# A four-layer graph network on one core: the first layer's neighbour sums made a stage earlier and kept in DRAM, a group's first layer moved to another stage, lists and zeros moved

## The chip, the core and the metric

The kernel runs on one NeuronCore of a Trainium2 chip. The core has five engines, each with its own in-order instruction queue: TensorE (PE in the profile; its weight loads are PEld), VectorE (DVE), ScalarE (ACT), GpSimd (POOL) and SyncE (SP). SP computes nothing here: it issues transfers. ACT and POOL issue transfers too. All transfers of the core share 16 DMA engines. The metric is the time of one execution in microseconds (us); lower is better. The time before is the median of three runs.

## The reference

There are 32 batch entries of 512 nodes with 256 features each, and one 512 x 512 weighted adjacency matrix that is mostly zero. Four layers follow one another. Layers 0 and 3 have the same form with other weights, and the changed sums belong to layer 0:

```python
x0 = layer(x, adj, weights of L0)
def layer(h_t, A_a, A_m, W1, b1, W2, b2, Wa, ba, Wm, bm, beta1, beta2, beta3):
    pre_u = jnp.einsum('bud,dk->buk', h_t, W1[:d])
    pre_v = jnp.einsum('bvd,dk->bvk', h_t, W1[d:])
    hidden = jax.nn.relu(pre_u[:, :, None, :] + pre_v[:, None, :, :] + b1)
    S = jax.nn.sigmoid(jnp.einsum('buvk,ko->buvo', hidden, W2)[..., 0] + b2[0])
    a_t = jnp.einsum('buv,bud->bvd', S * A_a, h_t)
    m_t = jnp.einsum('uv,bud->bvd', A_m, h_t) * h_t
    return beta1 * h_t + beta2 * (a_t @ Wa + ba) + beta3 * (m_t @ Wm + bm)
# layer 1: x + relu((adj @ x) @ W + b)
# layer 2: dense attention over 512 nodes with adj added to the logits, then x + values + bias
# layer 3: layer(...) again with the weights of L3
```

`S` is needed only where the adjacency is not zero. The quantity `adj.T @ h`, multiplied by `h`, is the neighbour sum `m_t`; the kernel calls it `mhT` (it is held transposed).

## The kernel before

**Groups and stages.** The 32 entries are worked on in eight groups of four (`NB`). For each group `t` there are five kinds of work, each a Python generator that yields after a small piece:

- `first` (L755): per entry, load x into `h` (a pool with two buffers, tag "h"), transpose it on TensorE (`turned`, L549) to `hT`, store that to DRAM as `xT` (issued by ACT), and make the two projections `pre_u` and `pre_v` (`pre`, L560: matmuls at L570 and L572, VectorE at L574, L577 and L578, ScalarE at L575). Each 128 rows of them go to a DRAM table (`table<-puv`, issued by SP through `settle`).
- `edges` (L611) for layer 0, later again for layer 3. There are 36 items (`ITEMS`), each 128 neighbour slots for the four entries of the group. Per item POOL gathers rows of the table (`fetch`, L607), VectorE adds them to the node's own rows (L686), applies relu and multiplies by W2 (L694 for all four entries at once, with ScalarE summing at L672; or L702 per entry with the sum in the same instruction). Every few items a sigmoid is taken, and POOL scatters the results into a zeroed DRAM matrix `cells` (`put`, L601), of which there are two halves. Each scatter waits until the one before it into the same half has landed.
- `middle` (L788, `middle_one` L825): load the four row blocks of the cells (`SA`, `load` at L721), then for each entry: `mhT` (matmuls in L45 and product at L750), the aggregation with the scattered weights (`flat` copied by ScalarE at L809, matmuls at L840), the product with Wm (L847), `zT` (scaled by ScalarE at L845, added by VectorE at L848), layer 1 (L861, L45), layer 2's attention (L883 to L953; the four matmuls of L899 come once per entry), and the first projections for layer 3 (`pre` again).
- `last` (L1016): layer 3's sums for the group, with its own `mhT` (tag "mhT3").
- In group 0 `middle_before` (L773) makes `hWa` and `mhT` of layer 0 ahead of the stage, and the last group has `last_before` and `last_behind`.

**The order.** The pieces of all generators are interleaved by a table of times written by hand in `sparse_path` (L1079): `spread` and `edge_times` give each piece a due time in units of one middle stage, and `weave` (L444) runs them in that order. Streams of kind "fill" (`first` and `last`) aren't run at their due time but collected, and one or two are run whenever the middle stage yields a true value, which it does where it is about to wait. The middle stage of group t takes the time t-0.47 to t+0.53. `behind` (L495) ties an instruction of the edges to a place in its engine's queue behind the middle stage's pieces; a scheduler then fixes each engine's order at build time.

**Setup.** `Edges.build` (L249) makes the lists of neighbours. Its last part (from L345) finds, for nodes with more than eight neighbours, the "panels": it reads the counts with matmuls, gathers four tiles `got` from the DRAM tensor `lists` by indirect transfers (L368), and searches them (L374, L377). `zeros` (L534) clears the cells of layer 0 and, called by `zeros_behind`, those of layer 3: each time eight stores of 512 KB from one zeroed tile.

**Buffers named below.** Tiles of one tag share memory: "h1" and "hT1" hold x and its transpose for the middle stage, "eT" the attention weights and `flat`, "mhT0" also `feats`, "hWa0" also `zW`. At both ends of the kernel, `edges` borrows further tags as extra row buffers (`rows_more`).

Of the kernel before, what the change touches and what calls it, by code (L numbers as in the profile page):

```python
# [8 lines left out]
F32 = mybir.dt.float32  # L9
# [210 lines left out]
class Edges:  # L220
# [28 lines left out]
    def build(self, counts, adjT, lists, psum, big, tmp):  # L249
# [65 lines left out]
        acc, v, there, t = (sheet(NC * OWN) for _ in range(4))  # L315
        for c in (0, 2, 1, 3):
            at = slice(c, c + 1)
# [27 lines left out]
        js = slice(NC * OWN, ITEMS)  # L345
        pu = psum()[:, 0 : 2 * PANELS]
        ones_bf = bf2[:, 1024:1025]
        nc.vector.memset(ones_bf, 1.0)
        for k in range(2 * PANELS):
            h, q = divmod(k, PANELS)  # L350
            mm(nc, pu[:, k : k + 1], [(full[:, h * 2 + c, q * P : (q + 1) * P], ones_bf) for c in range(2)])
        u, node, slot, start, sp, v, there, t = (sheet(2 * PANELS) for _ in range(8))
        nc.vector.tensor_scalar(u, pu, float(HALF - 1), None, ALU.min)
        nc.vector.tensor_copy(node, u)
        nc.vector.tensor_scalar(node[:, PANELS:], u[:, PANELS:], float(HALF), None, ALU.add)
        inode = self.inode
        nc.vector.tensor_copy(inode, node)
        nc.vector.tensor_scalar(self.iu, node, 2.0, None, ALU.mult)
        nc.gpsimd.iota(slot, [[0, 2], [P, PANELS]], 0, 1, allow_small_or_imprecise_dtypes=True)
        nc.vector.tensor_scalar(start, u, float(N), None, ALU.mult)  # L360
        nc.vector.tensor_scalar(sp, slot, float(CELLS + NC // 2 * OWN * P), None, ALU.add)
        nc.vector.tensor_scalar(t, slot, 1.0, None, ALU.add)
        yield
        gots = []
        for k in range(2 * PANELS):
            gots.append(tmp.tile([P, 2 * N], F32, name=f"got{k}", tag=("h1", "hT1", "mhT0", "hWa0")[k]))
            index = bass.IndirectOffsetOnAxis(ap=inode[:, k : k + 1], axis=0)
            nc.gpsimd.indirect_dma_start(out=gots[k], out_offset=None, in_=lists, in_offset=index)  # L368
        yield
        for k in range(2 * PANELS):  # L370
            at = slice(k, k + 1)
            rank, adj = gots[k][:, 0:N], gots[k][:, N:]
            junk = bf2[:, 2048 + k % 2 * N :][:, 0:N]
            nc.vector.scalar_tensor_tensor(  # L374
                junk, rank, t[:, at], adj, ALU.is_equal, ALU.mult, accum_out=self.value_of(NC * OWN + k)
            )
            nc.vector.scalar_tensor_tensor(junk, rank, slot[:, at], ones, ALU.is_le, ALU.mult, accum_out=v[:, at])  # L377
            yield
        self.slots(js, v, there, t, start, sp, 0)
        yield  # L380
# [34 lines left out]
class Sparse:  # L415
# [3 lines left out]
    def __init__(self, ctx, m, counts, xr, outr, B):  # L419
# [11 lines left out]

        self.xT, self.x2T = (self.dram.tile([B, P, DC, N], F32, name=n) for n in ("xT", "x2T"))
        self.e = Edges(m, pool("edges", 1))
        self.adjT = pool("adjT1", 1).tile([P, NC, N], F32, name="adjT")
# [94 lines left out]

    def zeros_behind(self):  # L530
        self.zeros(self.cells["3"])
        yield

    def zeros(self, cells):  # L534
        for c in cells:
            flat = c[0:CELLS, :].rearrange("(q p a) b -> q p (a b)", q=4, p=P)
            for q in range(4):
                self.nc.sync.dma_start(flat[q], self.zero)

# [215 lines left out]
    def first(self, g, i):  # L755
# [8 lines left out]
        for b in range(NB):  # L764
            ahead = load(b + 1) if b < NB - 1 else None
            hT = self.turned(h, "hT0", "hT")
            yield
            self.nc.scalar.dma_start(self.xT[i + b], hT)
            yield from self.pre(g, b, hT)
            h = ahead  # L770
        self.settle()

    def middle_before(self, g0, i):  # L773

        self.given = []
        for b in range(NB):
            h, hT = self.fresh(i + b)
            hT = hT()
            both = self.big(F32, 2048, 3).rearrange("p (k n) -> p k n", k=2)
# [8 lines left out]
    def middle(self, g0, g3, i):  # L788
# [3 lines left out]
        given, self.given = self.given, None  # L792
        h, hT = self.fresh(i, given)
        hT = hT()
# [5 lines left out]
        for b in range(NB):  # L800
            keep = [h, hT, hWa, flat]
            yield from self.middle_one(g0, g3, b, i + b, SA, keep, given)
            h, hT, hWa, flat = keep
        self.settle()
# [7 lines left out]
    def fresh(self, i, given=None):  # L812
        h = None
        if not given:
            h = self.act.tile([P, NC, D], F32, name="h1")
            self.nc.sync.dma_start(h, self.xr[i])

# [4 lines left out]

        return h, turned

    def middle_one(self, g0, g3, b, i, SA, keep, given):  # L825
        nc, m, w = self.nc, self.m, g0.w
        act, small, psum = self.act, self.small, self.psum
        h, hT, hWa, flat = keep
        if given:
            hWa, mhT = given[b]  # L830
        else:
            for mhT in self.mhT(h, hT, 0):
                yield
        zT = hT
# [208 lines left out]

FIRST, LAST, AHEAD, BEHIND = even(NB * 5 + 1), even(NB * 8 + 1), even(NB * 4 + 1), even(NB * 4 + 1)

# [17 lines left out]
def middle_shares(given):  # L1063
# [15 lines left out]
def sparse_path(ctx, m, counts, xr, outr, B):  # L1079
# [10 lines left out]
    for t in range(last + 1):  # L1090
# [17 lines left out]
        if t == last:  # L1108
# [254 lines left out]
```

## Time and profile before

| What | Value |
|---|---|
| Median of three runs | 3119.4 us (3118.76 to 3120.48) |
| The profiled execution's own time | 3102.14 us |
| Its span in the profile | 3100.4 us |
| Mean granted TensorE clock | 0.941 |
| Bytes read and written in HBM | 531.12 MB, 146.01 MB |
| TensorE busy, first 293.8 us | 163.3 us |
| TensorE busy, 293.8 to 885.4 us | 525.8 of 591.6 us |
| TensorE busy, 885.4 to 2650.7 us | 1658.9 of 1765.3 us |
| TensorE busy, 2846.2 us to the end | 195.7 of 254.2 us |

The profiled execution is one run with the hardware profiler; its own time lies 0.6% under the median. "Busy" is the time in which an engine has an instruction at work. A row of a stretch gives, for each engine, busy us and in brackets the number of instructions; the last three columns are the clock that TensorE was granted (1.00 is full), the mean busy share of the 16 DMA engines and the rate. A row of waits reads "engine line <- who released it: us in total, times, longest". In rows of groups and of the order of time, `out<-in` are names in the program, and the number after x is how many instructions are merged. One matmul of 32-bit numbers gives two records.

The chain that ended last, in the words of the profile, is 51% TensorE, 18% VectorE, 17% DMA, 6% issue, 4% ScalarE and 3% POOL.

### The profile page before, as it was taken

What the parts mean: (1) busy time and instruction counts of PE and PEld (TensorE: products, weight loads), DVE (VectorE), ACT (ScalarE), POOL (GpSimd) and SP (SyncE); (2) the same over time, 40 slices, a digit from 0 to 9 for tenths busy, and PEclk for the clock granted to TensorE, in tenths of its full rate; (3) what the DMA queues carried; (4) which work ended last, traced back from release to release, by engine and by line L of the source; (5) the groups of instructions that cost most, each with busy time, mean ns of one, the idle gap of its engine ahead of it and who ended that gap; (6) DMA issues with size and microseconds to landing.
All of it is one profiled execution on the core that took longest, in us unless ns stands there. A gap on an engine that the chain in (4) does not pass through costs nothing.

```text
span 3100.4 us, 32465 instructions
## 1 busy us (share of the span) xinstructions
PE 2714.6 (88%) x8645; PEld 1642.5 (53%) x8646; DVE 2302.8 (74%) x6026; ACT 1337.8 (43%) x4101; POOL 1522.5 (49%) x1312
## 2 busy tenths in 40 slices
PE   6366888889998999989998999989999899889957
PEld 3133444446654565546664565545664566545636
DVE  6783886889589875989589885888679795772761
ACT  3453554445345433545354442545335343453440
POOL 1462453556346563556346562565436563450561
PEclk9688988999999999999999999999999999999978
DMA  8874556786677766786668766787568766551753
GB/s 285 282 236 152 180 174 225 237 268 213 223 224 263 235 210 219 247 282 213 227 213 258 238 197 213 242 267 237 188 216 268 251 221 208 178 174 58 234 195 115
DMA packets 302719, 679.40 MB, mean 219 GB/s; under 512 B 52672, under 2 KB 170944, under 8 KB 294336
## 3 DMA queue, kind: packets, MB, share of 16 engines
q0 software_dynamic: 120384, 406.01, 41.0%
q1 hardware_dynamic: 163184, 234.01, 22.5%
q10 hardware_dynamic: 18960, 37.24, 3.2%
q8 instruction: 70, 1.15, 0.2%
q14 instruction: 121, 0.99, 0.1%
HBM read 531.12 MB, written 146.01 MB: 218 GB/s over the span
## 4 chain that ended last, share of the span: by engine, by line
PE 51%; DVE 18%; DMA 17%; issue 6%; ACT 4%; POOL 3%; SPq 0%; POOLq 0%; ACTq 0%; DVEq 0%
PE pst L45 24%; PE pst L1001 7%; DVE rows L686 6%; DMA table<-puv 5%; DMA rows<-table,iv 5%; PE pst L570 3%; DVE rows L702 3%; PE pst L861 3%; PE pst L1010 3%; PE pst L572 3%; DMA cells<-s,cell 3%; DVE rows L694 3%; PE pst L883 2%; PE pst L840 2%; DMA SA<-cells 2%
## 5 line engine op out<-in xcount | busy, mean ns | idle before, releaser
L601 POOL DMA_INDIRECT cells<-s,cell x576 | 691.1, 1200 | 740.7 <-DMA cells<-s,cell 370.3
L607 POOL DMA_INDIRECT rows<-table,iv x554 | 663.3, 1197 | 672.7 <-DMA table<-puv 148.1
L686 DVE TENSOR_TENSOR rows<-rows,mine 128x1024 f32<-128x1024 f32 x554 | 670.8, 1219 | 164.7 <-DMA rows<-table,iv 148.8
L672 ACT ACTIVATE rows<-rows 128x256 f32<-128x256 f32 x1096 | 442.9, 407 | 516.7 <-DVE rows L694 511.1
L45 PE MATMUL pst<-adj,h 128*128 128x512 f32 x1024 | 451.3, 592 | 0.3 <-PE pst L941 0.3
L702 DVE SCALAR_TENSOR_TENSOR rows<-rows,L_gnn_W2bc 128x256 f32<-128x256 f32 x1120 | 415.9, 419 | 1.8
L45 PE MATMUL pst<-L_gnn_Wa,hT 128*128 128x256 f32 x1024 | 264.3, 410 | 118.6 <-DMA hT<-xT 64.6
L694 DVE SCALAR_TENSOR_TENSOR rows<-rows,L_gnn_W2bc 128x1024 f32<-128x1024 f32 x274 | 332.3, 1216 | 0.3
L45 PEld LDWEIGHTS pst<-adj,h 128*128 128x128 f32 x1024 | 192.8, 190 | 222.4 <-issue 218.4
L45 PEld LDWEIGHTS pst<-L_gnn_Wa,hT 128*128 128x128 f32 x1024 | 207.7, 208 | 165.8 <-issue 53.1
L45 PE MATMUL pst<-eT,feats 128*128 128x512 f32 x512 | 231.5, 606 | 12.4 <-ACT eT L953 12.4
L45 PE MATMUL pst<-adjT,zW 128*128 128x512 f32 x512 | 227.8, 597 | 6.2 <-ACT zW L865 6.2
L1001 PEld LDWEIGHTS pst<-hWa,SA 128*128 128x128 f32 x896 | 213.7, 328 | 7.7 <-issue 4.5
L1001 PE MATMUL pst<-hWa,SA 128*128 128x256 f32 x896 | 216.8, 398 | 0.0
L861 PE MATMUL pst<-WT,hT 128*128 128x256 f32 x512 | 150.3, 459 | 75.9 <-DVE hT L848 75.9
L672 ACT ACTIVATION_READ_ACCUMULATOR rows<-rows 128x1 f32 x1096 | 206.7, 189 | 0.0
L809 ACT COPY flat<-SA 128x512 f32<-128x512 f32 x128 | 137.6, 1128 | 155.0 <-PE pst L45 60.1
L840 PE MATMUL pst<-flat,hWa 128*128 128x512 f32 x448 | 196.8, 592 | 0.0
L861 PEld LDWEIGHTS pst<-WT,hT 128*128 128x128 f32 x512 | 118.0, 235 | 114.9 <-DVE hT L848 88.1
L575 ACT COPY puv<-pst 128x256 f32<-128x256 f32 x256 | 93.7, 370 | 183.8 <-DVE puv L574 168.1
L574 DVE TENSOR_TENSOR puv<-pst,bc_L_gnn_b 128x256 f32<-128x256 f32 x256 | 105.0, 416 | 90.3 <-DMA table<-puv 53.8
L45 PEld LDWEIGHTS pst<-eT,feats 128*128 128x128 f32 x512 | 97.5, 193 | 127.5 <-issue 109.8
(170 smaller groups left out, 3979.3 us busy)
## 6 DMA issues: line engine op xcount, KB each, us to landing
table<-puv SPq DMA_DIRECT2D x256, 256.0 KB, 5.5
SA<-cells POOLq DMA_DIRECT2D x64, 1024.0 KB, 7.0
h<-in_x_dram SPq DMA_DIRECT2D x64, 512.0 KB, 6.4
mine<-table SPq DMA_DIRECT2D x64, 512.0 KB, 5.3
hT<-xT SPq DMA_DIRECT2D x36, 512.0 KB, 5.1
h<-x2s SPq DMA_DIRECT2D x36, 512.0 KB, 4.1
xT<-hT ACTq DMA_DIRECT2D x32, 512.0 KB, 5.5
x2T<-yT SPq DMA_DIRECT2D x32, 512.0 KB, 5.3
```

What stands on the lines that cost most here:

```text
L45: nc.tensor.matmul(out, lhsT, rhs, start=(n == 0), stop=(n == len(pairs) - 1))
L574: nc.vector.tensor_tensor(puv[:, 0, :], pp[:, 0:D], w["b1bc"], ALU.add)
L601: self.nc.gpsimd.indirect_dma_start(out=g.cells[half], out_offset=bass.IndirectOffsetOnAxis(ap=at, axis=0), in_=s, in_offset=None)
L607: self.nc.gpsimd.indirect_dma_start(out=rows, out_offset=None, in_=g.table, in_offset=bass.IndirectOffsetOnAxis(ap=at, axis=0))
L672: self.behind(nc.scalar.activation(part, part, AF.Identity, accum_out=g.s[:, k, b : b + 1]))
L686: self.behind(nc.vector.tensor_tensor(rows, rows, other, ALU.add))
L694: nc.vector.scalar_tensor_tensor(by_entry, by_entry, 0.0, w2, ALU.max, ALU.mult)
L702: nc.vector.scalar_tensor_tensor(part, part, 0.0, w["W2bc"], ALU.max, ALU.mult, accum_out=at)
L809: self.nc.scalar.copy(flat[:, r, :], SA[r][:, :, b])
L840: nc.tensor.matmul(pz, hWa[:, r, cs], flat[:, r, :], start=(r == 0), stop=False)
L861: nc.tensor.matmul(pw[:, at], zT[:, d, cs], m.WT_1[:, d, :], start=(d + k == 0), stop=(d * k == 1))
L1001: nc.tensor.matmul(pz[:, k * D : (k + 1) * D], SA[r][:, cs, b], hWa[:, r, :], start=(r + k == 0), stop=False)
```

## The change

It has five parts.

1. **Neighbour sums of layer 0.** `first` makes `mhT` for every group but group 0, just after storing `hT`, with the x tile it already holds, and SP stores it to a new DRAM tensor `mhTs`. `middle` no longer loads x and makes `mhT`; it loads `mhT` (`mhT1`, in tag "h1"). `first` uses tag "mhT3" for it. `middle_before` still makes its own. The table of times follows: `FIRST` has seven pieces an entry instead of five (group 0 keeps five), and `middle_shares` loses two.
2. **Group 2's `first`** is due from 0.1 to 0.45, in the middle stage of group 0, instead of 0.67 to 0.93 in that of group 1.
3. **The lists.** The panels' counts and the four gathers of `got` are made before the search of row block 1, not after all four. The tiles `got` use tags "eT" (two), "h1" and "hT1".
4. **The zeros.** All 16 zero stores are issued by POOL instead of SP, and those for layer 3 come after a fill of the zero tile by VectorE that is tied behind the middle stage.
5. **Row buffers.** Group 0's edges of layer 0 borrow "yT", "mhT0" and "hWa0" instead of "yT" and "mhT3": eight row buffers instead of seven.

```diff
@@ Edges.build
         for c in (0, 2, 1, 3):
+            if c == 1:
+                pu = psum()[:, 0 : 2 * PANELS]
...
+                for k in range(2 * PANELS):
+                    h, q = divmod(k, PANELS)
+                    mm(nc, pu[:, k : k + 1], [(full[:, h * 2 + c, q * P : (q + 1) * P], ones_bf) for c in range(2)])
...
+                yield
+                gots = []
+                two = tmp.tile([P, 2, 2 * N], F32, name="got", tag="eT")
+                for k in range(2 * PANELS):
+                    if k < 2:
+                        gots.append(two[:, k, :])
+                    else:
+                        gots.append(tmp.tile([P, 2 * N], F32, name=f"got{k}", tag=("h1", "hT1")[k - 2]))
+                    index = bass.IndirectOffsetOnAxis(ap=inode[:, k : k + 1], axis=0)
+                    nc.gpsimd.indirect_dma_start(out=gots[k], out_offset=None, in_=lists, in_offset=index)
+                yield
...
-            gots.append(tmp.tile([P, 2 * N], F32, name=f"got{k}", tag=("h1", "hT1", "mhT0", "hWa0")[k]))
...
@@ Sparse
+        self.mhTs = self.dram.tile([B, P, DC, N], F32, name="mhTs")
     def zeros_behind(self):
+        self.behind(self.nc.vector.memset(self.zero, 0.0))
         self.zeros(self.cells["3"])
         yield
...
-                self.nc.sync.dma_start(flat[q], self.zero)
+                self.nc.gpsimd.dma_start(flat[q], self.zero)
@@ first
             self.nc.scalar.dma_start(self.xT[i + b], hT)
+            if i > 0:
+                for mhT in self.mhT(h, hT, 3):
+                    yield
+                self.nc.sync.dma_start(self.mhTs[i + b], mhT)
             yield from self.pre(g, b, hT)
@@ fresh
-            h = self.act.tile([P, NC, D], F32, name="h1")
-            self.nc.sync.dma_start(h, self.xr[i])
+            mhT = self.act.tile([P, DC, N], F32, name="mhT1", tag="h1")
+            self.nc.sync.dma_start(mhT, self.mhTs[i])
@@ middle_one
-        h, hT, hWa, flat = keep
+        mhT, hT, hWa, flat = keep
         if given:
             hWa, mhT = given[b]
-        else:
-            for mhT in self.mhT(h, hT, 0):
-                yield
@@ the table of times
-FIRST, LAST, AHEAD, BEHIND = even(NB * 5 + 1), even(NB * 8 + 1), even(NB * 4 + 1), even(NB * 4 + 1)
+FIRST, LAST, AHEAD, BEHIND = even(NB * 7 + 1), even(NB * 8 + 1), even(NB * 4 + 1), even(NB * 4 + 1)
-        shares += [] if given else [2.8, 2.8]
-            first = spread(FIRST, -0.385, -0.30)
+            first = spread(even(NB * 5 + 1), -0.385, -0.30)
-            first = spread(FIRST, start - 0.86, start - 0.6)
+            first = spread(FIRST, 0.1, 0.45) if t == 2 else spread(FIRST, start - 0.86, start - 0.6)
-            (sp.edges(g0, ("yT", "mhT3") if t == 0 else ()), edges0, ""),
+            (sp.edges(g0, ("yT", "mhT0", "hWa0") if t == 0 else ()), edges0, ""),
```

More of the change, by code (lines that the diff above doesn't have):

```diff
@@ L316, in build @@
         for c in (0, 2, 1, 3):
+            if c == 1:
+                pu = psum()[:, 0 : 2 * PANELS]
+                ones_bf = bf2[:, 1024:1025]
+                nc.vector.memset(ones_bf, 1.0)
+                for k in range(2 * PANELS):
+                    h, q = divmod(k, PANELS)
+                    mm(nc, pu[:, k : k + 1], [(full[:, h * 2 + c, q * P : (q + 1) * P], ones_bf) for c in range(2)])
+                u, node, slot, start, sp, vp, therep, tp = (sheet(2 * PANELS) for _ in range(8))
+                nc.vector.tensor_scalar(u, pu, float(HALF - 1), None, ALU.min)
+                nc.vector.tensor_copy(node, u)
+                nc.vector.tensor_scalar(node[:, PANELS:], u[:, PANELS:], float(HALF), None, ALU.add)
+                inode = self.inode
+                nc.vector.tensor_copy(inode, node)
+                nc.vector.tensor_scalar(self.iu, node, 2.0, None, ALU.mult)
+                nc.gpsimd.iota(slot, [[0, 2], [P, PANELS]], 0, 1, allow_small_or_imprecise_dtypes=True)
+                nc.vector.tensor_scalar(start, u, float(N), None, ALU.mult)
+                nc.vector.tensor_scalar(sp, slot, float(CELLS + NC // 2 * OWN * P), None, ALU.add)
+                nc.vector.tensor_scalar(tp, slot, 1.0, None, ALU.add)
+                yield
[9 more added lines that the diff above has]
+                yield
             at = slice(c, c + 1)
@@ L343, in build @@
             yield
[L345 to L362, printed above, removed]
-        yield
-        gots = []
-        for k in range(2 * PANELS):
-            gots.append(tmp.tile([P, 2 * N], F32, name=f"got{k}", tag=("h1", "hT1", "mhT0", "hWa0")[k]))
-            index = bass.IndirectOffsetOnAxis(ap=inode[:, k : k + 1], axis=0)
-            nc.gpsimd.indirect_dma_start(out=gots[k], out_offset=None, in_=lists, in_offset=index)
-        yield
         for k in range(2 * PANELS):
@@ L374, in build @@
             nc.vector.scalar_tensor_tensor(
-                junk, rank, t[:, at], adj, ALU.is_equal, ALU.mult, accum_out=self.value_of(NC * OWN + k)
+                junk, rank, tp[:, at], adj, ALU.is_equal, ALU.mult, accum_out=self.value_of(NC * OWN + k)
             )
-            nc.vector.scalar_tensor_tensor(junk, rank, slot[:, at], ones, ALU.is_le, ALU.mult, accum_out=v[:, at])
+            nc.vector.scalar_tensor_tensor(junk, rank, slot[:, at], ones, ALU.is_le, ALU.mult, accum_out=vp[:, at])
             yield
-        self.slots(js, v, there, t, start, sp, 0)
+        self.slots(slice(NC * OWN, ITEMS), vp, therep, tp, start, sp, 0)
         yield
@@ L776, in middle_before @@
         for b in range(NB):
-            h, hT = self.fresh(i + b)
-            hT = hT()
+            h = self.act.tile([P, NC, D], F32, name="h1")
+            self.nc.sync.dma_start(h, self.xr[i + b])
+            hT = self.fresh(i + b, True)[1]()
             both = self.big(F32, 2048, 3).rearrange("p (k n) -> p k n", k=2)
@@ L792, in middle @@
         given, self.given = self.given, None
-        h, hT = self.fresh(i, given)
+        mhT, hT = self.fresh(i, given)
         hT = hT()
@@ L800, in middle @@
         for b in range(NB):
-            keep = [h, hT, hWa, flat]
+            keep = [mhT, hT, hWa, flat]
             yield from self.middle_one(g0, g3, b, i + b, SA, keep, given)
-            h, hT, hWa, flat = keep
+            mhT, hT, hWa, flat = keep
         self.settle()
@@ L812, in fresh @@
     def fresh(self, i, given=None):
-        h = None
+        mhT = None
         if not given:
-            h = self.act.tile([P, NC, D], F32, name="h1")
-            self.nc.sync.dma_start(h, self.xr[i])
+            mhT = self.act.tile([P, DC, N], F32, name="mhT1", tag="h1")
+            self.nc.sync.dma_start(mhT, self.mhTs[i])
         def turned():
@@ L821, in turned @@
             return hT
-        return h, turned
+        return mhT, turned
     def middle_one(self, g0, g3, b, i, SA, keep, given):
@@ L827, in middle_one @@
         act, small, psum = self.act, self.small, self.psum
-        h, hT, hWa, flat = keep
+        mhT, hT, hWa, flat = keep
         if given:
             hWa, mhT = given[b]
-        else:
-            for mhT in self.mhT(h, hT, 0):
-                yield
         zT = hT
```

## The prediction, made before the changed kernel was run

> **What bounds the kernel now.** First the page's busy shares: TensorE is busiest, but 12% of the span is idle, so the question is where.
>
> ```profile
> PE 2714.6 (88%) x8645; PEld 1642.5 (53%) x8646; DVE 2302.8 (74%) x6026; ACT 1337.8 (43%) x4101; POOL 1522.5 (49%) x1312
> PEclk9688988999999999999999999999999999999978
> ```
>
> Second, I cut the span at the 32 places where an entry's four L899 matmuls start (one per batch entry of the middle stage), and asked for each engine's busy time in each stretch. I call the stretches slot 0 (0 to 293.8) to slot 32. Columns: PE, PEld, DVE, ACT, POOL busy us (instructions), granted clock, DMA share, GB/s.
>
> ```profile
> 0.00:293.80 293.80, 163.25 (x461) 89.01 (x463) 183.58 (x453) 121.53 (x438) 121.53 (x118) 0.80 0.71 246
> 293.80:346.20 52.40, 44.12 (x133) 23.85 (x132) 43.29 (x113) 30.15 (x88) 16.70 (x14) 0.93 0.53 153
> 346.20:400.60 54.40, 43.70 (x133) 24.02 (x132) 46.31 (x119) 30.12 (x88) 31.01 (x27) 0.91 0.55 178
> 400.60:457.60 57.00, 47.39 (x134) 24.82 (x132) 46.21 (x138) 27.85 (x75) 29.95 (x28) 0.85 0.50 162
> ...
> 526.00:613.80 87.80, 79.45 (x239) 41.61 (x238) 79.33 (x216) 46.08 (x146) 52.12 (x44) 0.96 0.73 236
> 613.80:710.90 97.10, 78.45 (x230) 43.50 (x229) 79.48 (x230) 41.58 (x128) 55.46 (x48) 0.91 0.80 269
> 710.90:794.10 83.20, 83.20 (x294) 55.09 (x293) 72.11 (x191) 38.72 (x119) 53.55 (x44) 1.00 0.66 214
> 794.10:885.40 91.30, 90.54 (x309) 58.89 (x308) 55.31 (x141) 31.70 (x86) 31.77 (x29) 1.00 0.66 212
> 885.40:967.80 82.40, 78.00 (x245) 42.27 (x244) 76.75 (x206) 44.81 (x137) 48.72 (x41) 0.98 0.78 247
> 967.80:1059.00 91.20, 77.97 (x231) 44.14 (x230) 77.61 (x227) 40.04 (x123) 53.26 (x47) 0.94 0.78 270
> 1059.00:1142.20 83.20, 83.20 (x294) 55.10 (x293) 71.94 (x191) 39.11 (x119) 54.55 (x44) 1.00 0.67 214
> 1142.20:1235.50 93.30, 90.57 (x310) 58.89 (x309) 55.35 (x141) 31.73 (x86) 32.17 (x31) 1.00 0.65 209
> ```
>
> From slot 9 on a stage repeats every four slots, which I call A, B, C, D (A is 885.4 to 967.8); slots 9 to 28 hold five rounds. C and D are all TensorE. A is nearly all VectorE (76.75 of 82.4). B has 13 us of idle TensorE, slots 1 to 3 8 to 11 us each, slot 0 130.
>
> Third, the waits and TensorE's order of time in slot B show its stall: the last scatters of the old group's edges each wait for the one before to land, gathers queue behind them on POOL, VectorE stands at L686, and TensorE waits for `hT`.
>
> ```profile
> POOL cells L601 <- DMA cells<-s,cell: 24.3, 11, 4.7
> PE pst L861 <- DVE hT L848: 6.5, 1, 6.5
> ```
>
> Fourth, prices in TensorE's order of time. Start to start, a 16-record product over 512 columns takes 6.86 us:
>
> ```profile
> 918.56 7.03 PE L45 MATMUL pst<-adj,h 128*128 128x512 f32 x16
> 925.42 7.03 PE L840 MATMUL pst<-flat,hWa 128*128 128x512 f32 x16
> ```
>
> One entry's neighbour sum is 6.87 us; its first layer is 6.9 us (L570, L572) plus 0.9 (eight transposes, L556).
>
> **The change, part by part.** The changed kernel's built order, cut at the same matmuls, says what each slot holds; priced by these rows at full clock, TensorE's work changes by: slot 0 +27.5 us (group 1's sums: 4 x 6.87); slots 1, 2, 3 +15.5, +24.9, +18.1 (group 2's first layer and sums); 4 to 8 -7.7, -30.1, -17.5, -3.1, -8.6; A +18.9, B -7.2, C -3.1, D -8.6 (next group's 27.5 us arrives, four sums of the own group leave); 29 to 31 -6.9, -6.9, -8.6. It sums to zero: nothing is removed, so all gain is idle time filled.
>
> Slot 0. SP's eight zero stores (12.93 us of issue from 23.86) leave its queue. VectorE's first `puv` part is written at 27.86 and ScalarE's half at 28.31, yet the first table store goes at 38.14; so 0 to 9.4 us, cut by the x load behind it (TensorE waits 6.2 us for it at 50.56): 6. On POOL these eight precede L313, needed only by the panel matmuls at 109.5: covered, else 8 x 1.2 (the indirect rows) = 9.6. The four list gathers (138.15 to 143.19 on the chain) move before the first table gathers: up to 5 saved, 3 taken. The second eight zero stores (4.2 MB) leave the busiest DMA stretch (share 0.88 between 60 and 120 us); four stores of sums (2.1 MB) come in: no net cost. Added: eight L750 products x 0.68 = 5.4 us of VectorE, which is 58.6 of 80 us busy between 120 and 200: 1 taken; the matmuls lie in TensorE's 130 idle us. Sum -8, bounds -20 and +5.
>
> The Trainium skill, "DMA: Bandwidth & Descriptors", section "Issuing engines are not separate DMA queues", speaks against this: another issuing engine saves only sequencer issue time, usually small beside the transfer. Here eight issues took 12.93 us against a median landing of 7.3; by the rule the term would be near 0 and the total 6 us higher.
>
> Slots 1 to 3. Work at full clock is 40.8 us each, so becomes 56.3, 65.7, 58.9 = 181 against 163.8 now. Bounds: +17 (all idle used, full clock) and +58 (none). VectorE gains 12 first-layer operations (0.41 each) and 2 to 4 products a slot, about 7 us on 46: covered. The moved zero stores come here after a VectorE fill of 1.2 us (as L686); they hold POOL up to 9.6 us, which is 16.7 of 52.4 busy in slot 1; behind them stand group 1's scatters, so uncovered it is +9.6. I take +24, near the lower end: the pieces are inserted where the stage waits.
>
> "TensorE: Matmul & The Clock Gate", Part 1 of the skill: an idle array falls to half clock until it has worked a few microseconds. The rows agree: 0.93, 0.91, 0.85 here, 1.00 in C, and busy time exceeds full-clock work by 12.8 us in the three slots. With the rule in full, filling them returns the 12.8; with none of it returned the term would be about +35.
>
> Slot 4 (68.4 us, 52 of work, falling to 44): it waits for group 1's last scatters and the SA loads, which now have longer cover: -8, bounds -24 and 0.
>
> Slots 5 and 6. TensorE drops to 98.7 us; VectorE loses 16 `puv` and 32 `both` operations, 48 x 0.41 = 20 us of 158.8. It then bounds: 139 us at today's 86% busy gives 161 for 184.9. Bounds -45 and 0 (the scatter chain as in B); taken -24. Slot 7: full, -3. Slot 8: -8.6 if TensorE bounds, 0 if the SA load does; -4.
>
> Slots A to D, five times. A: 94.1 of work for 82.4, so +12 at least, +18.9 if nothing overlaps; VectorE's four more products (2.7) are covered; +14. B: -7.2 of work that stood before the stall, so the stall may merely grow; but the slot begins with VectorE less behind, and fewer new-group edges stand ahead of `hT` in VectorE's built order; bounds -26 and 0, taken -9. C -3. D -5 (bounds -8.6 and 0, the SA load). Sum -3 a round, -15; bounds -20 (all of a round's idle time) and +16 (A in full, C alone back).
>
> The 28 stores of 512 KB add 14.7 MB to 679.4 (2%) where shares are 0.5 to 0.8; the load of sums replaces the load of x one for one. SP waits in front of each store for VectorE's product, and behind it stand the next table stores and prefetches; those need later work of the same pieces, so 0. If that cover is gone, a prefetch is late by half a sum, 3.4 us, four times a round: 14, which A's upper bound holds.
>
> Slots 29 to 31: 22 us of work leave slots 9 to 17 us from full; -9 (bounds -22, 0). The end after 2846 is unchanged.
>
> Sum: -8 +24 -8 -24 -7 -15 -9 = -47. It is made against the profiled execution, 3102.1 us (span 3100.4), 0.6% under the shown median 3119.4; taken off the median it gives 3072.
>
> **The rivals.**
> 1. Slower. The sums make slot A TensorE's own bound (+14.6) and nothing returns it: B still ends with the scatter chain (24.3 us of waits, idle TensorE instead of work before it) and D with the SA load; only C gives 3. That is +11.6 a round, 58 for five, in place of -15: 3119.4 - 32 + 58 = 3145. It decides from +6.4 a round. For it: slots 20 and 24 already last 98.6 and 98.4 us with TensorE idle, so those chains are near. Against it: VectorE had no slack in A and gets some. Chance 0.20.
> 2. Small gain: slots 1 to 3 overlap badly (+40) and 5 and 6 stay on the scatter chain (-10): -47 + 16 + 14 = -17, 3102. For it: in slots 1 to 3 TensorE waits behind single softmax steps that a 3.4 us piece overshoots; against it: the pieces stand at just these waits. Chance 0.17.
> 3. Large gain: B's stall goes (-16 there, -10 a round), slot 0 gives 18: -47 - 35 - 10 = -92, 3027. Its condition is a shorter scatter tail, for which only VectorE's lead speaks. Chance 0.12.
> 4. The pieces sit elsewhere at run time than in the built order: each engine keeps its order, so only 0.03, near 3119.
>
> **How the numbers follow.** My forecast, 0.48, is 3072, with its own range 3045 to 3098. Both signs: 3020 to 3138 holds eight in ten, reaching most of rival 1. A difference under 0.2% (6 us) can't be told from none here. Faster 0.72 (forecast, rivals 2 and 3, less their edges), same 0.05, slower 0.23 (rival 1 and the forecast's and rival 2's far ends).
>
> **What would show it.** In the changed profile: the first table store near 30 us; `got` gathers before the first `rows`; the first slot starting near 286; slots 1 to 3 at 58 to 70 us with clock near 1.0; slots 5 and 6 together near 160; A near 96 with TensorE full, B 80 to 85, C 80, D 85 to 90. I am wrong if B stays at 90 with more TensorE idle before L861 (rival 1), or SP's waits at the new store hold up hT or table transfers.

## The result and the profile after

The changed kernel took 3139.8 us (median of four runs, 3129.6 to 3142.4) where the kernel before took 3119.1 on the same chip (four runs). The ratio is 1.006, with a 95% interval from 1.0037 to 1.0083: slower by 0.6%, where 1.5% faster was forecast. The profiled execution has a span of 3127.8 us, 27.4 over that of before.

These are the page's two lines of the changed kernel that answer to those shown of before:

```profile
PE 2720.7 (87%) x8645; PEld 1644.8 (53%) x8646; DVE 2299.5 (74%) x6027; ACT 1326.5 (42%) x4101; POOL 1552.2 (50%) x1328
PEclk9788999889999999999999999999999999989978
```

TensorE has the same instructions (x8645). It is busy 6.1 us longer with them, at a mean granted clock of 0.933 in place of 0.941; the other 21 us of the 27.4 are idle time. The span cut at the same matmuls (now L907) shows where; columns as before, slots 0 to 3, 5, 6 and the first round:

```profile
0.00:285.79 285.79, 190.41 (x525) 102.69 (x527) 187.28 (x461) 121.04 (x438) 130.81 (x126) 0.84 0.73 246
285.79:354.00 68.21, 61.07 (x182) 32.76 (x181) 50.79 (x137) 32.90 (x95) 19.46 (x22) 0.92 0.69 222
354.00:422.03 68.03, 66.06 (x199) 34.07 (x198) 53.33 (x140) 35.11 (x98) 37.16 (x32) 1.00 0.72 229
422.03:492.56 70.53, 62.47 (x182) 32.43 (x181) 54.34 (x161) 29.61 (x81) 27.93 (x25) 0.95 0.56 185
...
551.56:627.14 75.58, 51.26 (x149) 29.30 (x148) 68.57 (x173) 39.04 (x128) 51.09 (x42) 0.84 0.64 197
627.14:718.02 90.88, 64.37 (x182) 36.30 (x180) 68.82 (x203) 37.83 (x119) 54.01 (x49) 0.80 0.75 248
...
893.96:990.04 96.08, 94.93 (x294) 49.93 (x292) 83.84 (x224) 46.29 (x147) 50.63 (x43) 1.00 0.75 247
990.04:1075.89 85.85, 70.66 (x206) 37.96 (x204) 64.91 (x196) 35.40 (x105) 43.87 (x39) 0.92 0.79 264
1075.89:1160.80 84.91, 80.75 (x293) 55.47 (x292) 78.56 (x202) 42.01 (x135) 59.08 (x47) 1.00 0.66 214
1160.80:1256.25 95.45, 84.44 (x285) 56.11 (x284) 53.94 (x146) 30.10 (x78) 37.25 (x33) 0.93 0.62 208
```

Slot A is now full of TensorE work. Slot D, which was nearly full (90.57 busy of 93.30), is 2 us longer with 84.44 of work in it: 11 us of TensorE stand idle there. Slot B holds 15 us of idle TensorE, where it held 13.

The waits of that slot B (us in total, times, longest) name a new one. TensorE's L891 waits for `yT`, which VectorE makes behind edges that wait for gathered rows (its L880 at 1065.16 follows row waits of 7.6 and 3.8 us):

```profile
DVE rows L692 <- DMA rows<-table,iv: 16.1, 4, 7.6
PE pst L891 <- DVE yT L880: 9.2, 2, 8.2
```

Over the five slots B, VectorE's waits for these gathers grew from 46.8 to 78.8 us, and TensorE's for `yT`, 4.5 in the whole run before, came to 44.5. Older waits shrank there: for `hT` from 27.2 to 7.7, for the softmax's `ex` from 19.0 to 12.7. In all TensorE stood idle for 74.0 us in these five slots, 70.2 before: the stall moved, it hardly grew.

Over the five slots D, a wait of TensorE ahead of `hWa` that was not there before comes to 44.7 us. The profile names no releaser for it ("issue"); the order of time of slot D points to one (start, duration, engine, then the idle time before it):

```profile
1178.82 1.16 POOL L733 DMA_DIRECT2D SA<-cells  x2 [1.43 <-DMA cells<-s,cell]
1180.28 1.01 POOL L607 DMA_INDIRECT cells<-s,cell  x1 [0.30 <-issue]
1189.47 1.01 POOL L607 DMA_INDIRECT cells<-s,cell  x1 [8.18 <-DMA cells<-s,cell]
1192.37 0.97 POOL L607 DMA_INDIRECT cells<-s,cell  x1 [1.89 <-DMA cells<-s,cell]
1195.21 0.96 POOL L607 DMA_INDIRECT cells<-s,cell  x1 [1.87 <-DMA cells<-s,cell]
1198.06 1.16 POOL L733 DMA_DIRECT2D SA<-cells  x2 [1.89 <-DMA cells<-s,cell]
...
1203.13 1.09 ACT L820 COPY flat<-SA 128x512 f32<-128x512 f32 x1 [12.97 <-DMA SA<-cells]
1204.12 0.37 ACT L581 COPY puv<-pst 128x256 f32<-128x256 f32 x1
...
1205.05 6.06 PE L45 MATMUL pst<-L_gnn_Wa,hT 128*128 128x256 f32 x16 [11.02 <-issue]
```

In the kernel before the same pair of loads, `hWa` and the entry's own neighbour sum stood so:

```profile
1165.35 1.14 POOL L727 DMA_DIRECT2D SA<-cells  x2 [1.42 <-DMA cells<-s,cell]
1176.83 3.62 PE L45 MATMUL pst<-L_gnn_Wa,hT 128*128 128x256 f32 x16
1180.29 7.03 PE L45 MATMUL pst<-adj,h 128*128 128x512 f32 x16
```

The second pair of SA loads is issued 37.3 us after the slot's start (1160.80); before, it was 23.2 (start 1142.20). In the changed kernel ScalarE, in order, stands at `flat` until they land, and the copies of `puv` out of PSUM stand behind it; TensorE goes on 0.9 us after the first of them. Before, the sum of this slot came behind `hWa`; so it can't have covered this wait, and the later load is what is new.

The whole change by slots, in us of the profiled executions: slot 0 -8.0; 1 to 3 +43.0; 4 -9.4; 5 and 6 -18.4; 7 and 8 +1.5; a round +6.3 (A +12.6, B -5.8, C +0.4, D -0.9), five rounds +31.2; 29 to 31 -16.1; the end +4.0.

### The profile page after: what moved, and what is told of

It is laid out like the page before. It is cut to its first block, busy times and chain, and to the rows that moved or that the text cites. A ratio compares the mean times of both kernels' runs of the same rounds, so it can differ in the third digit from the quotient of the medians.

```text
span 3127.8 us, 32431 instructions
## 1 busy us (share of the span) xinstructions
PE 2720.7 (87%) x8645; PEld 1644.8 (53%) x8646; DVE 2299.5 (74%) x6027; ACT 1326.5 (42%) x4101; POOL 1552.2 (50%) x1328
## 4 chain that ended last, share of the span: by engine, by line
PE 41%; DVE 27%; DMA 16%; issue 7%; ACT 5%; POOL 3%; POOLq 0%; ACTq 0%; DVEq 0%; SPq 0%
PE pst L45 18%; DVE rows L692 8%; DMA table<-puv 7%; PE pst L1009 6%; DMA rows<-table,iv 4%; DVE rows L700 4%; DVE rows L708 4%; PE pst L848 3%; PE pst L1018 2%; PE pst L576 2%; PE pst L869 2%; PE pst L891 2%; PE pst L578 2%; ACT rows L678 2%; DMA cells<-s,cell 2%
## 5 line engine op out<-in xcount | busy, mean ns | idle before, releaser
L607 POOL DMA_INDIRECT cells<-s,cell x576 | 723.1, 1255 | 674.0 <-DMA cells<-s,cell 367.8
L692 DVE TENSOR_TENSOR rows<-rows,mine 128x1024 f32<-128x1024 f32 x552 | 665.1, 1214 | 215.6 <-DMA rows<-table,iv 207.3
L45 PE MATMUL pst<-adj,h 128*128 128x512 f32 x1024 | 460.4, 597 | 3.3 <-DVE both L583 3.3
L45 PE MATMUL pst<-L_gnn_Wa,hT 128*128 128x256 f32 x1024 | 279.2, 425 | 139.9 <-issue 53.6
L45 PEld LDWEIGHTS pst<-L_gnn_Wa,hT 128*128 128x128 f32 x1024 | 218.1, 218 | 189.0 <-issue 104.3
L45 PE MATMUL pst<-eT,feats 128*128 128x512 f32 x512 | 242.8, 630 | 16.1 <-ACT eT L961 16.1
L583 DVE TENSOR_TENSOR both<-pst,puv 128x256 f32<-128x256 f32 x256 | 107.1, 418 | 118.1 <-ACT puv L581 110.7
L891 PE MATMUL pst<-WT,yT 128*128 128x257 f32 x512 | 137.7, 425 | 61.5 <-DVE yT L880 61.5
```

Source lines behind the costliest of these rows:

```text
L45: nc.tensor.matmul(out, lhsT, rhs, start=(n == 0), stop=(n == len(pairs) - 1))
L583: nc.vector.tensor_tensor(both, pp[:, D:], puv[:, 0, :], ALU.add)
L607: self.nc.gpsimd.indirect_dma_start(out=g.cells[half], out_offset=bass.IndirectOffsetOnAxis(ap=at, axis=0), in_=s, in_offset=None)
L692: self.behind(nc.vector.tensor_tensor(rows, rows, other, ALU.add))
L891: nc.tensor.matmul(pn[:, 0 : D + 1], yT[:, r, ic * P : (ic + 1) * P], m.WT_2[:, r, :], start=(r == 0), stop=(r == DC - 1),)
```

## The experiments

The later runs fell on other chips, where the kernel before took 3122 to 3133 us and single executions spread over 20 to 40 us; so they are told as ratios to the kernel before on the same chip, with the 95% interval. Slot lengths in us from the profiles; A to D are means over five rounds. Among the kernels of the later chips the rounds are measured against e2, whose rounds hold the same pieces as those of the kernel before.

| kernel | ratio | 0 | 1-3 | 4-8 | A | B | C | D | round | 29-31 |
|---|---|---|---|---|---|---|---|---|---|---|
| before (first chip) | 1 | 293.8 | 163.8 | 427.8 | 82.7 | 92.9 | 83.2 | 94.3 | 353.1 | 195.6 |
| e5 changed, again | 1.0048 | 284.0 | 207.3 | 408.1 | 94.9 | 90.6 | 83.9 | 93.9 | 363.3 | 179.8 |
| e2 head alone | 0.9966 | 281.3 | 170.5 | 434.9 | 83.9 | 93.9 | 83.2 | 95.9 | 356.9 | 196.6 |
| e9 free sums | 0.9983 | 285.2 | 203.8 | 402.5 | 81.1 | 98.9 | 83.5 | 93.3 | 356.8 | 179.0 |
| e15 changed, lead 4 | 0.9961 | 280.8 | 207.5 | 396.0 | 94.8 | 77.1 | 90.1 | 94.2 | 356.2 | 178.5 |
| e16 and move undone | 0.9909 | 282.9 | 170.2 | 424.7 | 95.0 | 80.4 | 89.9 | 94.0 | 359.3 | 180.9 |
| e17 and earlier tail | 0.9852 | 280.6 | 169.5 | 425.4 | 95.4 | 89.6 | 80.2 | 88.2 | 353.4 | 178.9 |
| e18 e17, no sums | 0.9903 | 281.9 | 167.7 | 431.9 | 83.4 | 96.2 | 84.0 | 90.0 | 353.6 | 198.5 |

**First four: which part costs what.** `e1_g2_back` undoes one line:

```diff
-            first = spread(FIRST, 0.1, 0.45) if t == 2 else spread(FIRST, start - 0.86, start - 0.6)
+            first = spread(FIRST, start - 0.86, start - 0.6)
```

> The changed kernel with the third group's first layer put back to its old place, one stage later. Theory 1 (the move is a loss: slots 1 to 3 grew by 43 us and slots 4 to 6 gave back only 28): slots 1 to 3 return to about 164 us, slots 5 and 6 become a round's A and B and gain about 6 over before; total 9 us under the changed kernel, near 3131. Rival (the move is a gain as predicted, -8 net, and the loss lies wholly in the rounds): total 8 us over the changed kernel or more, 3148. In both the rounds stay at +6 each.

Measured: 1.0006 (0.9986 to 1.0025). The changed kernel itself has 1.0048 (e5 below, on another of the later chips), so the move costs 0.42%, about 13 us, give or take 8; theory 1 had 9. Slots 5 and 6 went from 169 to 186, as its account has it.

`e2_head_only` takes the changed kernel and undoes the sums and the move; lists, zeros and row buffers stay.

> The kernel before with the lists' gathers early, the zero stores on POOL and the other row buffers, and without the sums and without the third group's move. If slot 0's -8 is due to these three parts and is kept: 3119 - 8 = 3111. Rival (the -8 came with TensorE being kept busy by group 1's sums, or is given back in slot 1): 3119.

Measured: 0.9966 (0.9940 to 0.9992), -10.6 us. The head's gain is there without the sums. Which of its three parts gives it was not separated.

`e3_no_sums` is e2 with the move:

```diff
-            first = spread(FIRST, start - 0.86, start - 0.6)
+            first = spread(FIRST, 0.1, 0.45) if t == 2 else spread(FIRST, start - 0.86, start - 0.6)
```

> The changed kernel without the sums ahead (each entry makes its own sum in the middle stage again), with the third group's first layer in the first middle stage and the head's parts. Theory 1 (in the rounds the sums bunch in slot A, and slots B and D end with chains that lose TensorE's cover): rounds return to 350 us each, so about 31 us under the changed kernel, 3105 to 3112. Rival (the rounds got slower for another reason than the sums): near 3140.

Measured: 1.0008 (0.9989 to 1.0028). The move alone costs 0.42% over e2, as in e1; the sums alone (e1 over e2) cost 0.40%. With -0.34% of the head the three parts add up to the changed kernel's +0.48%. The rounds returned to 356.8, e2's length, 6.5 under those of e5, so the rounds' loss is the sums'. The total missed both expectations: it lies about 0.4% under the changed kernel, where theory 1 had 1%.

`e4_old_times` keeps the middle stage's times, with gaps for the sums:

```diff
+        shares += [] if given else [-2.8, -2.8]
         shares += [3.4, 3.4, 1.0, 2.7]
...
-        times.append(a + (b - a) * at / sum(shares))
-        at += share
+        if share > 0:
+            times.append(a + (b - a) * at / total)
+        at += abs(share)
```

> The changed kernel, but the times of the middle stage's pieces kept as before, with gaps where the sums stood; only the order of pieces changes. Theory 2 (dropping the sums' shares moved the stage's marks 0.012 of a stage earlier against the edges, so the scatter tail and the second pair of SA loads come 11 us later in slot D): the second SA pair moves from +35 back towards +25 us in D, D shrinks by 5 to 8 us a round, total 3100 to 3115. Theory 1: the SA loads move little, total 3133 to 3145.

Measured: 1.0094 (1.0056 to 1.0131). The first half of theory 2 held: the second SA pair went from +35 to +23 us after D's start. The second half fell: D kept 92.8 us, with waits of TensorE for `hT` (17.4 us over five) and `hWa` (10.2) in place of the one wait, and B grew to 93.7. Moving all pieces of the stage together moved the wait and didn't remove it.

**Next four: cover or chain.** `e5_after_again` is the base on this chip.

> The changed kernel itself, on the same chip as the next three, as their base. Expected 0.4 to 0.9% over the kernel before; slot A 94 to 96 us, C within 2 us of 83, D 92 to 96.

Measured: 1.0048 (1.0031 to 1.0066). Its slots are those of the first chip within 6 us.

`e6_own_first` has the first entry's sum made in the middle stage again:

```diff
-            if i > 0:
+            if i > 0 and b > 0:
...
+        elif b == 0:
+            for mhT in self.mhT(mhT, hT, 0):
+                yield
```

> The changed kernel with the sum of each group's first entry (b = 0) made in the middle stage again, where it stood before, and only entries 1 to 3 ahead. Theory 1 (A is full on TensorE, and in D the removed sum left a hole while ScalarE waits for the SA load): A loses 5 to 7 us, D keeps its length within 1.5 us with TensorE busy again near 90; five rounds and slot 5 give 25 to 40 us under the changed kernel, below the kernel before. Rival (a sum costs its 6.9 us wherever it stands): A -6, D +6, no change against the changed kernel.

Measured: 1.0134 (1.0109 to 1.0159), slower than the changed kernel; both expectations missed. D grew by 5.5 to 99.4, the sum's work, and TensorE's wait ahead of `hWa` was still 5.8 us a round: the sum stands behind `hWa` in TensorE's order and can't cover it. A grew to 102.8 with less work in it, with new waits of TensorE for VectorE's `both` (24.6 us over five); why stays open.

`e7_no_chain_after` and `e8_no_chain_before` send three of four scatters to arrays that nobody reads, by this edit in the two kernels:

```diff
-            out=g.cells[half], out_offset=...
+            out=self.turn(g, half), out_offset=...
...
+    def turn(self, g, half):
+        self.puts += 1
+        k = self.puts % 4
+        return self.others[half][k - 1] if k else g.cells[half]
```

> The changed kernel with its scatters going in turn to four cell arrays, three of which nobody reads, so that no scatter waits for the one before it and the SA loads wait only for every fourth; the edge values in three of four scatters are lost. Theory 1 (slots B and D end with the scatter chain): the waits of scatters on scatters go to nearly nothing, B falls from 86 to 89 to about 75 and D from 93 to 95 to 85 to 87, so 15 to 20 us a round, 75 to 110 in all; it comes to the time of the kernel before without the chain within 15 us, or below it. Rival (the loss does not need the chain): it stays at least 18 us over the kernel before without the chain.

> The kernel before with the same edit (scatters in turn to four cell arrays, three of which nobody reads; those edge values are lost). Theory 1: B falls from 91 to 95 to about 80, C stays at 83.2, D loses at most 3 us (it was nearly full of TensorE work), so 10 to 15 us a round, 50 to 75 in all, less than the changed kernel gains by the same edit. Rival: both kernels gain the same within 10 us.

Measured: 0.9642 (0.9615 to 0.9669) and 0.9611 (0.9585 to 0.9636). Slots A to D are 95.1, 80.1, 84.9, 85.0 and 81.4, 87.4, 83.2, 90.0. So the waits for landed scatters, of the next scatters and of the SA loads, are worth 3.9% in the kernel before, and B and D depend on them: in the changed kernel they fall by 10.5 and 8.9 us, in the kernel before by 5.5 and 4.3. But against their own times the two kernels gain nearly alike (4.1% and 3.9%), as the rival of e8 has it; theory 1 had 50 to 75 us for the kernel before, which gained 121. The shorter chain by itself doesn't turn the moved work into a gain.

**The sums for nothing.** `e9_free_sums` leaves out the products, TensorE's and VectorE's, and their places in the table of times; the stores, with the turned entry in them, and the loads stay.

```diff
-                for mhT in self.mhT(h, hT, 3):
-                    yield
-                self.nc.sync.dma_start(self.mhTs[i + b], mhT)
+                self.nc.sync.dma_start(self.mhTs[i + b], hT)
...
```

> The changed kernel without the eight products of each sum: the first layer stores the turned entry in the sums' place, so all its stores, loads, moves and times stay and 27.5 us of TensorE work a round and 5.4 of VectorE are left out. Theory 1 (the sums were independent work that TensorE did while an entry's own chain ran; taken out of B, C and D they leave waits): A returns to 82 to 86 us, while B, C, D stay at 86 to 91, 82 to 85 and 92 to 95, so a round is only 6 to 12 us shorter than before for 27.5 us less work; total 3060 to 3090. Rival (the slots follow TensorE's work): the round falls by 20 us or more under before, total under 3000. Second rival (the extra stores and loads are the cost): A stays above 90.

Measured: 0.9983 (0.9956 to 1.0009). Theory 1 had a total of 3060 to 3090 us, the rival less still; neither came. TensorE has 27.5 us less to do in a round, and the round, 356.8 us, is as long as e2's 356.9. Against e5 A falls by 13.8 and B grows by 8.3. The waits of slot 14 (a slot B) show what B is made of:

```profile
DVE rows L692 <- DMA rows<-table,iv: 18.0, 5, 8.6
DVE puv L580 <- DMA table<-puv: 8.8, 3, 3.6
```

VectorE waits for gathers and table stores, 26.8 us of 100.8. Over the five slots B its waits for gathers are as long as in e5 (89.6 us for 91.9) and those for table stores longer (35.8 for 14.1). So most of what TensorE's lighter A gave was lost again in B, where TensorE waits for VectorE.

`e10_ends_only` makes the sums ahead for the second and the last group alone:

```diff
-            if i > 0:
+            if self.made(i):
...
+    def made(self, i):
+        return i // NB in (1, self.last_group)
```

> The changed kernel with the sums ahead only for the second group (made in the head) and the last group (whose own middle stage has no next group's first layer beside it), the third group's first layer back at its old time; the middle groups make their own sums again. Theory 1 (a moved sum gains only where TensorE stands idle when it is made, or where the slot it leaves is not refilled): the head's parts give -10, the second group about -8, the last group about -7, the four rounds between return to 350 to 354; ratio to the kernel before 0.990 to 0.994. Rival (sums moved gain nothing anywhere): 0.9966, that of the head's parts alone.

Measured: 1.0024 (1.0001 to 1.0047), a miss. Against e2, slot 4 gave 4.5 us and slots 5 to 8 took 5.6; the last group's sums cost 17.3 in slots 25 to 28 and returned 14.4 in 29 to 31.

`e11_first_wider` starts the first layer earlier:

```diff
-            first = spread(FIRST, 0.1, 0.45) if t == 2 else spread(FIRST, start - 0.86, start - 0.6)
+            first = spread(FIRST, 0.1, 0.45) if t == 2 else spread(FIRST, start - 0.98, start - 0.6)
```

> The changed kernel with the next group's first layer begun 0.12 of a stage earlier, from the fourth group on, so that one entry's first layer and sum go from slot A to slot D (A 78.6 instead of 94.1 us of TensorE work, D 97.0 instead of 81.5). Theory 1 (bunching in A is the cost, and D has 9 us of TensorE waiting): A falls by 10 to 15, D grows by 4 to 9, so 4 to 8 us a round, 20 to 40 in all, ratio 0.994 to 1.001. Rival (D's wait is not filled by pieces that stand behind it in TensorE's order): D grows by 13 to 16, A falls as much, ratio 1.003 to 1.008.

Measured: 1.0197 (1.0163 to 1.0231). D grew by 15.5 us, all of the work put there, and its 9.2 us wait stayed, as the rival had it; A returned only 9.7. The loss is past the rival's 0.8% too.

**What else is on the chain.** `e12_free_no_chain` joins the edits of e7 and e9.

> Both edits at once: the sums' products left out (the turned entry is stored in their place) and the scatters in turn to four cell arrays, three of which nobody reads. Theory 3 (a round is set by the edges' chain of gathers and scatters; TensorE's work only counts where it is longer than that chain, in slot A of the changed kernel): with the chain shortened the left-out 27.5 us a round count at last, A falls under 82, B to 75 to 80, the round from 345 to 318 to 330, total 2830 to 2920, ratio 0.905 to 0.935. Rival (another chain of the entry itself, softmax and VectorE, sets the round): 335 to 345 a round, total 2960 or more, ratio over 0.945.

Measured: 0.9566 (0.9531 to 0.9600); a round 341.3. Against e7, 27.5 us less work gave 3.8 a round. So even with the scatter waits shortened TensorE's amount of work doesn't set the round; VectorE still waits 137.7 us over five rounds for gathers. The rival, another chain, is nearer, and what that chain is was not settled.

`e13_free_no_store` leaves out the 28 stores too:

```diff
-                self.nc.sync.dma_start(self.mhTs[i + b], hT)
+                pass
...
-            self.nc.sync.dma_start(mhT, self.mhTs[i])
+            self.nc.sync.dma_start(mhT, self.xT[i])
```

> As the free sums, and also without the 28 stores of 512 KB; the middle stage loads the turned entry where it would load the sums. Theory 3: the stores are not on the edges' chain; the ratio stays at 0.995 to 1.001 as with the free sums. Rival (the stores, by SP's queue and the DMA engines, made the round of the free sums as long as before's in spite of 27.5 us less TensorE work): 0.97 to 0.985, with slot B under 92 and VectorE's waits for table stores and gathers down by a third or more.

Measured: 0.9939 (0.9915 to 0.9962), 0.44% or 14 us under e9, give or take 11: between the two expectations. A round is 2.7 us shorter. VectorE's waits for table stores in B fall from 35.8 to 22.7 us over five.

`e14_lead_head` and `e15_lead_after` change one constant, in e2 and in the changed kernel:

```diff
-LEAD = 3
+LEAD = 4
```

> The head's parts alone with the edges' gathers four items ahead of their use and not three (the fifth row buffer is there already). Theory 3 (VectorE's waits for gathers in slot B, 9 to 18 us a round, are part of the chain): B falls by 3 to 8 us a round, ratio 0.984 to 0.992 against 0.9966 without it. Rival (the gathers stand behind scatters that wait for one another, so an earlier place in the queue gains nothing): 0.994 to 0.999.

> The changed kernel with the gathers four items ahead. Theory 3: VectorE's wait for gathers in B (15.8 us a round) is longer here than in the kernel before (9.4), so it gains at least as much as the head's parts alone: ratio 0.990 to 0.999 against 1.005. Rival: 1.002 to 1.008.

Measured: 0.9932 (0.9907 to 0.9957) and 0.9961 (0.9941 to 0.9980). The changed kernel gains 0.87%, as theory 3 has it; e2 0.34%, between the two expectations. Its round, slots 13 to 16:

```profile
1241.55:1335.82 94.27, 94.27 (x294) 50.07 (x293) 84.07 (x225) 46.69 (x149) 51.26 (x42) 1.00 0.78 250
1335.82:1413.68 77.86, 69.34 (x206) 36.88 (x204) 60.94 (x185) 35.14 (x103) 40.14 (x37) 0.96 0.79 269
1413.68:1503.74 90.06, 83.11 (x294) 57.02 (x293) 82.75 (x214) 42.07 (x135) 64.82 (x50) 0.96 0.69 219
1503.74:1597.58 93.84, 83.88 (x285) 55.59 (x284) 53.65 (x144) 30.32 (x78) 34.40 (x32) 0.95 0.66 214
```

B is 13.5 us shorter than in e5 on average, C 6.2 longer, the round 7.1 shorter. VectorE's waits for gathers over the five slots fall from 91.9 to 50.5 us in B and grow from 9.7 to 32.3 in C.

**Slot D, and a kernel that beats both.** `e16_lead_g2_back` is e15 with e1's line.

> The changed kernel with the gathers four items ahead and the third group's first layer at its old time: the head's parts and the sums, without the move. If the parts add (the move cost 0.4% in e1 and e3, four items ahead gave 0.9% here): ratio 0.990 to 0.994, level with or below the head's parts with four items ahead (0.9932). Rival (slots 5 and 6 then carry a round's A and B again and give it back): 0.995 to 0.999.

Measured: 0.9909 (0.9880 to 0.9939): the parts add. Against e14 (0.9932) the sums no longer cost anything, though the intervals are too wide to call it a gain.

`e17_tail_earlier` adds to it:

```diff
-            edges0 = edge_times(start - 0.552, start - 0.505, start - 0.06, start - 0.04)
+            edges0 = edge_times(start - 0.552, start - 0.505, start - 0.085, start - 0.065)
```

> As the kernel above, and the edges' items of the middle groups end 0.025 of a stage (9 us) earlier, so that the last scatters and the SA loads come earlier in slot D. If D's 9 us of TensorE waiting is the late SA load: the second SA pair goes from +35 to about +27 us after D's start, TensorE's wait before hWa falls from 10 to under 3 us, D from 94 to about 87; 25 to 40 us in all, ratio 0.980 to 0.986. Rival (as with the old times in e4, an earlier SA load only shows other waits): D 91 or more or B longer by as much, ratio 0.989 to 0.997.

Measured: 0.9852 (0.9820 to 0.9884), 3084.4 us against 3132.0 of before. TensorE's only wait in slot 16 (a slot D), first in e16, then in e17:

```profile
PE pst L45 <- issue: 8.5, 1, 8.5
```

```profile
PE pst L45 <- issue: 3.1, 1, 3.1
```

The second SA pair is issued at 24.4 us of the slot, not 34.4; D falls from 94.0 to 88.2, as expected, though not to 87. Over the five slots D that wait falls from 47.7 to 20.7 us. B grows by 9 and C falls by 10: those two trade, and the round is 5.9 us shorter.

`e18_tail_no_sums` is e17 without sums and move.

> The head's parts with the gathers four items ahead and the edges' items ending 0.025 of a stage earlier, without the sums ahead and without the move: e17 without the sums. If moving the sums pays once the edges' chain is out of the way: ratio 0.990 to 0.994 (D was nearly full of TensorE work with the own sum in it, so an earlier SA load gives it little), over e17's 0.9852. Rival (the gain of e17 is the earlier tail's alone and the sums' move is worth nothing): 0.982 to 0.988.

Measured: 0.9903 (0.9875 to 0.9932), as the first reading has it, though the intervals of e17 and e18 overlap a little. A round is the same in both (353.4, 353.6); what the sums give e17 lies outside the rounds, 19.6 us of it in slots 29 to 31.

## Why the prediction was wrong, by its own steps

**Slots A to D (predicted -3 a round, measured +6.3; 46 us of the 74 between forecast and profile).** A +14 was right (+12.6). What failed is the return: "B: -7.2 of work that stood before the stall, so the stall may merely grow ... taken -9", "C -3", "D -5". B, C and D gave 6.3 together. TensorE's busy time fell there by 6.5, 2.2 and 7.0 us a round; B became 5.8 shorter, C 0.4 longer, D 0.9 shorter. So B gave back its work, but not the stall (14.0 us idle before, 14.8 after), which I had let shrink. C and D gave back next to nothing: I had read a slot full of TensorE work as a slot set by TensorE. C now holds 2.6 us of waits for VectorE, D the 9 us ahead of `hWa`. e9 shows the same of the whole round: 27.5 us less of TensorE's work in it bought nothing against e2. Two places were then shown by moving the edges alone: with one gather more ahead B fell by 13.5 us and the round by 7.1 (e15), with an earlier tail D fell by 5.8 and the round by 5.9 (e17). Rival 1 named the mechanism for D, "B still ends with the scatter chain ... and D with the SA load"; it erred in size (+11.6), since B did give 5.8, and its sign, more idle time before L861, did not come: that wait shrank and another took its place.

**Within D**, "bounds -8.6 and 0, the SA load" was right at its upper end, but I took the SA load's time as given. The change cuts the sums' shares out of the stage's list of times, and so moves the other pieces against the edges: the second SA pair came at 33 to 37 us of the slot in place of 22 to 26, and with the old times it came at 21 to 26 again (e4), which cut the wait ahead of `hWa` to 10.2 us over five slots but brought 17.4 for `hT`. The diff showed the dropped shares; I costed only the work.

**Slots 1 to 3 (+24, measured +43).** "The pieces are inserted where the stage waits" failed. TensorE's idle time in the three slots fell only from 28.6 to 17.1 us, and of the 12.8 us lost to the clock some 4 came back (busy 189.6 us for 181 of work at full clock; granted 0.92, 1.00 and 0.95, where I had looked for near 1.0): 15.5 of 58.5 absorbed, nearer the bound of +58 for none than that of +17. The largest wait left, 5.7 us at L960 for VectorE's softmax step, is a single one; that the added pieces stand elsewhere in TensorE's order and so can't fill such waits is my reading, no run shows it. Slots 4 to 8 returned 26 where 39 was taken; slot 8, a slot D, has the late SA load too (34.7 us after its start, 22.1 before). The move of the third group is a loss of 0.4% (e1, e3).

**The 28 stores (0, or 14 a round with the cover gone).** e13 against e9 gives 14 us in the whole kernel (0.44%, each ratio to +-0.25%), 2.7 a round in the profiles: not free, and far from the 14 a round. This was measured with the products left out.

**Right:** slot 0, -8.0, to the digit; the head's parts alone gave -10.6 us (e2). The single terms were not separated, so the close hit is in part luck. Of the four list gathers one went ahead of the first rows (75.58 and 78.71), the other three behind four row gathers (83.99 to 86.49), not all ahead as forecast. The eight zero stores held POOL for 4.41 us of issue, where I had priced 9.6. By the Trainium skill ("DMA: Bandwidth & Descriptors", "Issuing engines are not separate DMA queues") another issuing engine saves only issue time, which is usually small. The first table store, behind 12.93 us of zero stores in SP's queue before, went at 28.77 in place of 38.14: here the issue time was not small, though no run shows what it alone gave. Slot 4 (-9.4 for -8); slots 29 to 31 gave more, -16.1 for -9. Slots 5 and 6 gave -18.4 for -24, with 27 us of waits left for `yT` and `hT`. The end, which I took as unchanged, grew by 4.0: the work changes listed in the prediction sum to -3.4 us and not to zero, and the rest, eight more TensorE records, stands there.

**Open:** what floor A and B share when the scatters don't wait and the sums are gone (172 us in e12); why A grew in e6; what holds C at its length. How the stores cost 14 us, by SP's queue or by the DMA engines, was not separated.

## What to carry to other kernels

A slot in which one engine is busy throughout is not thereby set by that engine: before moving work out of it, ask which chain of transfers and in-order engines ends just after. Here C and D lost 9 us of TensorE work a round and kept their length, while slot A, where the work went, grew by 12.6 for 16 us of it. When pieces leave a hand-timed schedule, all other pieces shift against one another, so re-time the loads that the next stage waits for in the same change. Here undoing the third group's move, one gather more ahead and a tail 9 us earlier turned +0.5% into -1.5%. The same kernel without the sums stands at -1.0% (e18), so their share is about 0.5%, at the edge of the noise and outside the rounds. Leaving the moved work out altogether is a cheap first experiment: it tells how far the time follows that work with the schedule as it stands.

## What the hardware showed unasked

A wait can cost more than its length. In e4's slot 14 TensorE's 16-record product over 512 columns, 7.03 us when it follows other work, took 9.98 after a wait of 4.31, and 7.03 again further on:

```profile
1379.46 9.98 PE L45 MATMUL pst<-eT,feats 128*128 128x512 f32 x16 [4.31 <-ACT eT L961]
...
1397.02 7.03 PE L848 MATMUL pst<-flat,hWa 128*128 128x512 f32 x16
```

The clock granted to TensorE was 0.71 over the first of these and 1.00 over the second, and 7.03 / 0.71 is 9.9. In slot 16 of the same kernel one took 8.83 us after a wait of 3.02, at 0.81. Shorter waits need not do this: the seven such products of e9 that follow a wait of 1.5 to 2.5 us took 7.13 to 7.14. Nor does the last wait alone decide: in slot B of the changed kernel one took 9.14 after a wait of 0.86, with one of 3.57 shortly before. With the sums left out, the mean granted clock of the run fell from 0.929 (e5) to 0.911 (e9). And a scatter issued right behind two SA loads of 1 MB on POOL's queue held the next one for 5.5 to 8.2 us in the changed kernel (six slots D), where the scatters after it in the slot shown waited 1.9.
